# Fifth stage of a two-layer decoder: exponentials of the two key halves are added before the product with the column of ones

## The chip, the cores and the metric

The kernel runs on one core of a Trainium2 chip. Times are device microseconds of one launch; the time of a kernel is the median of its runs. Engines are called TensorE (PE in the profile; PEld is its loading of weights), VectorE (DVE), ScalarE (ACT), GpSimd (POOL) and SyncE (SP, which only issues transfers here).

## The reference

Two decoder layers, six steps, over x of 8 batches of 256 tokens and 256 features in fp32; each step adds its result to x and normalises. Steps 1, 2, 4 and 5 are attention with 16 heads of 16 features (1 and 5 differ in masks; 2 and 5 take keys and values from a context), step 3 is a mixture of four experts, step 6 of eight. The change is in step 5:

```python
logits = jnp.einsum('bhqd,bhkd->bhqk', q, k) / jnp.sqrt(jnp.asarray(dh, q.dtype))
logits = logits + neg[:, None, :, :]
attn = jax.nn.softmax(logits, axis=-1)
attn = attn * group_prob[:, None, :, :]
out = jnp.einsum('bhqk,bhkd->bhqd', attn, v)
```

The softmax is divided by the sum of its exponentials over the 256 keys *before* the product with group_prob. So two things are summed over keys for each head and query: exponential x group_prob x value (16 features), and the plain exponential (the divisor).

## The kernel before, in words

**Stages.** An Item (40 of them) is one batch in one of the five attention or projection stages; the fifth stage is items 32 to 39. Per item there are two groups g of 8 heads, and per group two parities par of 4 heads r. All matrices are fp32 unless a name says bf16.

**One group of the fifth stage.** score_rows makes scores with queries on the partitions; VectorE reduces them to row maxima (mrow), max_rows turns these with TensorE and folds them into q. weights(it, g, par) then makes scores with keys on the partitions: two tiles res[0], res[1] of [128, 2, 512] (tag pt, 6 buffers), each with two heads; the 512 columns of a head are 256 queries for the first 128 keys, then 256 queries for the second 128 keys. ScalarE writes the exponentials into them. In this stage alone (it.masked), each tile is multiplied by the group probabilities (it.gT, part of the tile mg) into a tile pw, in two instructions of 128x1024, each on VectorE or GpSimd.

values(it, g, par) sums over the keys in PSUM (av_ps, read later as avT). TensorE is used in four columns of 32 (mode "columns"), one head r in each. For both key halves kc and the four heads, pw meets the values in vaug (8 products of 256 queries). Then, in this stage, the bare exponentials p meet onesel, a [128, 32] matrix that is 1 in column 16 and 0 elsewhere, and add the divisor to the same PSUM tile: again 2 key halves x 4 heads, 8 products. In the other stages the ones sit in vaug beside the values and no such products are needed. After both parities VectorE transposes (avT), takes the reciprocal (ri) and VectorE or GpSimd multiplies (on); a second transpose gives oT for the output projection.

**What sets the order.** Program records every operation (note, and pe for a group of TensorE instructions that stay together), with the engines that may run it: either("vector", "gpsimd") leaves the choice open. order() then lays out the whole kernel as a list: it follows a simulated clock with its own durations (function duration, lines 238 to 255; columns for TensorE), gives next what can start first, and picks for each operation the engine that is expected to end it first, with LEAN = 0.5 us added to VectorE's end. Among TensorE operations that could start within a short wait, the one of lowest rank goes; the rank is a due time, moved a little by a table of numbers, DRAWS: one number for each stretch of 25 us of due time, which seeds random shifts and chooses the hold (a penalty for changing the array's mode) and the wait of that stretch. Each engine executes its part of the list in order. Every recorded instruction shows as line 394 (or 419) in the profile, so groups are told apart by their tiles.

**Queues and neighbours.** In the fifth stage GpSimd also runs on, the bias of the residual (res), small steps of the layer norm, the masks (mg from mi) and the scatters of finished rows to slots, which the sixth step's experts load; these begin before the stage ends (xeT, h, w in the profile). SyncE issues all loads.

Of the kernel before, what the change touches and what calls it, by code (L numbers as in the profile page):

```python
# [21 lines left out]
ALU = mybir.AluOpType  # L22
# [6 lines left out]
B, S, D = 8, 256, 256  # L29
# [16 lines left out]
AHEAD, HOLD, LEAN, WAIT = 500, 1.0, 0.5, 0.6  # L46
STRETCH = 25.0
DRAWS = (
    4492, 0, 1957, 1835, 1496, 0, 91, 5789, 2392, 5451, 5841, 3357, 6082, 1933, 4381, 1902, 4765,
    2407, 5027, 1409, 0, 3899, 0, 1034, 0, 0, 1677, 2696, 3561, 1043, 3249, 1318, 5799, 5442, 4785,  # L50
    5199, 1355, 3729, 1195, 1519, 1668, 942, 4299, 0, 0, 0, 0, 0,
)
TURN, SWITCH, SIGNAL, EARLY, RATE = 0.11, 0.2, 0.12, 40.0, 0.35e6

# [8 lines left out]
def columns(n, count=1):  # L63

    return count * n * 1.69e-3
# [208 lines left out]
class Program:  # L274
# [160 lines left out]
    def _close(self, op):  # L435
# [25 lines left out]
        op.pre.discard(op.idx)  # L461
        op.behind -= op.pre | {op.idx}

    def order(self):

        ops = self.ops
# [37 lines left out]

        rank_of, hold, wait = list(due), [HOLD] * len(ops), [WAIT] * len(ops)
        draws = {k: random.Random(1000 * k + n) for k, n in enumerate(DRAWS) if n}
        for op in ops:
            k = int(due[op.idx] // STRETCH)  # L510
            if k in draws:
                n = DRAWS[k]
                rank_of[op.idx] += (0.25, 0.5, 1.0, 2.0)[n % 4] * (2.0 * draws[k].random() - 1.0)
                hold[op.idx] = (0.5, 1.0, 2.0, 4.0)[n // 4 % 4]
                wait[op.idx] = (0.2, 0.3, 0.6, 1.0)[n // 16 % 4]
        left = [len(op.pre) + len(op.behind) for op in ops]
        begun = [0.0] * len(ops)
        end = [None] * len(ops)
# [1 line left out]
        ready = [i for i, n in enumerate(left) if n == 0]  # L520
        oldest, result = 0, []
        self.clock = []

        def places(op, now):

# [36 lines left out]
        def division(op):  # L562

            if op.mode == "any":
                return ("columns" if mode == "rows" else mode or "full",) * 2
            if op.mode == "rows, full":
                return ("full", "rows") if mode == "full" else ("rows", "full")
            return op.mode, op.mode

        while ready:  # L570
            choices = []
            for i in ready:
                op = ops[i]
                if i > oldest + AHEAD:
                    continue
                here = places(op, free.get(op.alts[0][0], 0.0))
                if here is None:
                    continue
                t0 = max([here[0]] + [begun[p] for p in op.behind])
                opts = []  # L580
                for e, f, d in op.alts:
                    t = t0
                    for p in op.pre:
                        if ops[p].ran != e or ops[p].lag:
                            t = max(t, end[p] + SIGNAL + (0.15 if ops[p].mode else 0.0))
                        else:
                            t = max(t, end[p])
                    t = max(t, free.get(e, 0.0))
                    if e == "sync":
                        t = max(t, due[i] - EARLY)  # L590
                    if e == "all":

                        t = max(free.values())
                    if op.mode:
                        first, then = division(op)
                        d += SWITCH * ((first != mode) + (first != then))
                    opts.append((t + d + (LEAN if e == "vector" else 0.0), t, d, e, f))
                fin, t, d, e, f = min(opts, key=lambda o: o[:3])
                rank = rank_of[i] + (hold[i] if op.mode and division(op)[0] != mode else 0.0)
                choices.append((t, rank, i, op, d, e, f, here[1]))  # L600
            if not choices:
                raise RuntimeError(f"operation {oldest} of {len(ops)} cannot be given")
            best = min(choices, key=lambda c: c[:3])
            if best[3].mode:

                best = min(
                    (c for c in choices if c[3].mode and c[0] <= best[0] + wait[best[2]]), key=lambda c: c[1:3])
            t, _, _, op, d, e, f, found = best
            i = op.idx
            if op.mode:  # L610
                first, then = division(op)
                op.split, op.flip = op.mode == "any" and first == "columns", (first, then) == ("full", "rows")
                mode = then
            op.ran = e
            if e == "all":
                for k in free:
                    free[k] += d
            else:
                free[e] = t + d
            begun[i], end[i] = t, t + d  # L620
            if op.lag:
                wire = max(wire, t + d + 1.3) + op.bytes / RATE
                end[i] = max(t + d + op.lag, wire + 0.9)
            for b, where in zip(op.new, found):
                for n in where:
                    lanes[b.key][n] = b
                b.at = where[0]
                taken[b.key] += not b.loose
            ready.remove(i)
            for j in op.post + op.ahead:  # L630
                left[j] -= 1
                if left[j] == 0:
                    ready.append(j)
            while oldest < len(ops) and (end[oldest] is not None or ops[oldest].alts[0][0] == "sync"):
                oldest += 1
            result.append(f)
            self.clock.append((t, t + d, e, i))
        return result


@with_exitstack
def decoder_kernel(ctx: ExitStack, tc: tile.TileContext, a: dict, out: bass.AP):
# [552 lines left out]
    def weights(it, g, par):  # L1195

        ps = [psum_s("st_ps") for _ in range(2)]
        res = [work.tile([P, 2, 512], F32, tag="pt", name="pt", bufs=6) for _ in range(2)]
        with nc.pe(columns(S, 1.75 if it.causal else 2) + (0.9 if it.masked else 0.0), "rows", res):
            for kc in range(2):  # L1200
                q0 = P if (it.causal and kc == 1) else 0
                for r in range(4):
                    rows32 = slice(32 * r, 32 * r + 32)
                    nc.tensor.matmul(
                        ps[r // 2][:, r % 2, kc * S : kc * S + S - q0],
                        lhsT=it.k[par][rows32, g, kc * P : (kc + 1) * P], rhs=it.q[par][rows32, g, q0:],
                        start=masks_last if it.masked and kc == 0 else not it.masked,
                        stop=masks_first if it.masked and kc == 1 else not it.masked,
                    )
            if it.masked:  # L1210
                with nc.whole():
                    for r in range(4):
                        nc.tensor.matmul(
                            ps[r // 2][:, r % 2, :], lhsT=identb, rhs=it.mk.rearrange("p k q -> p (k q)"),
                            start=masks_first, stop=masks_last,
                        )
        n = S + P if it.causal else 2 * S
        for t, p in enumerate(res):
            nc.scalar.activation(p[:, :, :n], ps[t][:, :, :n], AF.Exp)
            if it.causal:  # L1220
                d = p.rearrange("p r (b x) -> p r b x", b=2)[:, :, :, :P]

                nc.gpsimd.affine_select(
                    out=d, in_=d, compare_op=ALU.is_ge, fill=0.0, base=0,
                    pattern=[[0, 2], [0, 2], [1, P]], channel_multiplier=-1,
                )
        it.p[g, par] = res
        if it.masked:
            w = big("pw").rearrange("p (t r x) -> p t r x", t=2, r=2)
            gb = it.gT.rearrange("p k q -> p (k q)").unsqueeze(1).to_broadcast([P, 2, 512])  # L1230
            for t in range(2):
                nc.either("vector", "gpsimd").tensor_tensor(w[:, t], res[t], gb, ALU.mult)
            it.pw[g, par] = [w[:, 0], w[:, 1]]

    def values(it, g, par):
# [3 lines left out]
        ps = it.av  # L1239
        p = it.p.pop((g, par))  # L1240
        w = it.pw.pop((g, par)) if it.masked else p
        with nc.pe(columns(S, (1.5 if it.causal else 2) * (2 if it.masked else 1)), "columns"):
            for kc in range(2):
                q0 = P if (it.causal and kc == 1) else 0
                for r in range(4):
# [4 lines left out]
                        start=(kc == 0), stop=(kc == 1 and not it.masked),  # L1250
                    )
            if it.masked:
                for kc in range(2):
                    for r in range(4):
                        nc.tensor.matmul(
                            ps[32 * r : 32 * r + 32, par, :], lhsT=onesel,
                            rhs=p[r // 2][:, r % 2, kc * S : (kc + 1) * S], start=False, stop=(kc == 1),
                        )
        if par == 1:
            return  # L1260
        t = own_tile("avT", [P, 2, 8, 32], bufs=1)
# [990 lines left out]
```

## Time and profile before

| What | us |
|---|---|
| Median of 3 runs (lowest to highest) | 1420.42 (1420.22 to 1422.8) |
| The profiled execution, device time | 1426.34 |
| Its span, first to last instruction | 1424.3 |
| TensorE busy in the span | 1338.7 |
| VectorE busy | 903.0 |
| ScalarE busy | 618.9 |
| GpSimd busy | 598.5 |
| Fifth stage: first and last product with onesel begin at | 1029.5 and 1254.9 |
| Mean granted TensorE clock (a share of full speed) | 0.982 |

A group's line gives engine, operation, written tile <- read tiles, the shape (partitions x elements) and the count, then busy us, mean ns of one, and the engine's idle time just before such instructions with what ended it. A timeline's line gives start and length in us, engine, operation and count, with idle time before it in brackets. A stretch's line gives its bounds and length, then busy us and records (x) of each engine. Ends of matmuls are modelled and their spans overlap the next ones', so starts are the surer measure.

### The profile page before, as it was taken

What the parts mean: (1) busy time and instruction counts of PE and PEld (TensorE: products, weight loads), DVE (VectorE), ACT (ScalarE), POOL (GpSimd) and SP (SyncE); (2) the same over time, 40 slices, a digit from 0 to 9 for tenths busy, and PEclk for the clock granted to TensorE, in tenths of its full rate; (3) what the DMA queues carried; (4) which work ended last, traced back from release to release, by engine and by line L of the source; (5) the groups of instructions that cost most, each with busy time, mean ns of one, the idle gap of its engine ahead of it and who ended that gap; (6) DMA issues with size and microseconds to landing.
All of it is one profiled execution on the core that took longest, in us unless ns stands there. A gap on an engine that the chain in (4) does not pass through costs nothing. (4 is left out here: it accounts for less than half of the span.)

```text
span 1424.3 us, 34194 instructions
## 1 busy us (share of the span) xinstructions
PE 1338.7 (94%) x14418; PEld 907.7 (64%) x14448; DVE 903.0 (63%) x1813; ACT 618.9 (43%) x968; POOL 598.5 (42%) x979
## 2 busy tenths in 40 slices
PE   8999999999999988999899979999999999999995
PEld 5777666666666655757565645556566666577774
DVE  5777888778878875000230669987767878964332
ACT  3546575655655434222231354646443344432120
POOL 3446542314454665100260446672345556552222
PEclk9999999999999989999999989999999999999998
DMA  2210010400190013200320000021003103176500
GB/s 88 69 34 14 11 48 18 164 1 2 62 406 32 32 35 108 78 15 17 88 72 24 16 19 26 24 75 44 11 17 115 51 17 112 53 209 199 163 14 13
DMA packets 60753, 92.48 MB, mean 65 GB/s; under 512 B 6482, under 2 KB 49491, under 8 KB 59568
## 3 DMA queue, kind: packets, MB, share of 16 engines
q1 hardware_dynamic: 55792, 78.78, 17.0%
q0 software_dynamic: 4800, 11.41, 2.5%
q8 instruction: 118, 1.93, 0.6%
q14 instruction: 43, 0.35, 0.1%
HBM read 58.56 MB, written 32.28 MB: 64 GB/s over the span
## 5 line engine op out<-in xcount | busy, mean ns | idle before, releaser
L394 ACT ACTIVATE pt<-banks 128x1024 f32<-128x1024 f32 (+1 forms) x320 | 283.3, 937 | 226.0 <-PE banks L394 206.9
L394 DVE TENSOR_REDUCE mrow<-banks 128x4 f32<-128x1024 f32 (+1 forms) x320 | 342.6, 1109 | 58.9 <-PE banks L394 56.8
L394 PE MATMUL banks<-q,k 32*128 32x256 f32 (+1 forms) x2560 | 185.5, 382 | 11.1 <-PEq L343 5.0
L394 PE MATMUL banks<-k,q 32*128 32x256 f32 (+1 forms) x2560 | 187.3, 379 | 8.3 <-DVE mrow L394 6.8
L394 PEld LDWEIGHTS banks<-q,k 32*128 32x128 f32 x2560 | 128.3, 187 | 66.6 <-issue 39.5
L394 PEld LDWEIGHTS banks<-k,q 32*128 32x128 f32 x2560 | 129.3, 187 | 56.1 <-issue 20.2
L394 PE MATMUL banks<-pt,vaug 128*32 128x256 f32 (+1 forms) x2048 | 118.0, 361 | 4.5 <-DVE mrow L394 2.6
L394 POOL TENSOR_SCALAR_AFFINE_SELECT pt<-pt 128x512 f32<-128x512 f32 x128 | 81.4, 642 | 93.5 <-ACT pt L394 90.6
L394 POOL TENSOR_TENSOR on<-avT,ri 128x256 f32<-128x256 f32 x56 | 35.3, 631 | 180.2 <-DVE ri L394 147.6
L394 POOL TENSOR_TENSOR pw<-pt,mg 128x1024 f32<-128x1024 f32 x29 | 75.5, 2604 | 62.6 <-ACT pt L394 62.4
L394 PEld LDWEIGHTS banks<-pt,vaug 128*32 128x32 f32 x2048 | 58.8, 110 | 52.5 <-issue 14.9
L394 POOL DMA_INDIRECT got<-answers,where x32 | 31.2, 975 | 144.5 <-DMA xr<-sent 124.3
L394 PE MATMUL banks<-hid,big 128*128 128x512 f32 (+1 forms) x240 | 86.8, 521 | 0.0
L394 PE MATMUL banks<-xe,big 128*128 128x512 f32 (+1 forms) x216 | 82.4, 538 | 1.1 <-DVE xe L394 1.1
L394 ACT ACTIVATE hid<-banks 128x1024 f32<-128x1024 f32 (+1 forms) x39 | 34.3, 881 | 112.3 <-PE banks L394 112.2
L394 DVE STREAM_TRANSPOSE avT<-banks 128x512 f32<-128x512 f32 x80 | 56.8, 710 | 32.0 <-PE banks L394 22.3
L394 PE MATMUL banks<-xeT,w 128*128 128x320 f32 (+2 forms) x352 | 72.3, 362 | 1.8 <-DVE h L394 1.8
L394 DVE TENSOR_SCALAR xe<-banks,c_cols 128x512 f32<-128x512 f32 (+1 forms) x8 | 4.9, 613 | 108.8 <-PE banks L394 108.8
L394 PE MATMUL banks<-w,h 128*128 128x256 f32 (+1 forms) x384 | 72.2, 381 | 1.2 <-ACT h L394 1.2
L394 DVE SCALAR_TENSOR_TENSOR q<-banks,c_cols,q 128x256 f32<-128x256 f32 x160 | 69.0, 469 | 2.4 <-PE banks L394 2.2
L394 PEld LDWEIGHTS banks<-hid,big 128*128 128x128 f32 x240 | 45.5, 190 | 38.9 <-issue 36.8
L394 POOL TENSOR_SCALAR is_t<-ln_mv 128x2 f32<-128x2 f32 (+1 forms) x64 | 12.6, 197 | 133.9 <-DVE ln_mv L394 126.2
(247 smaller groups left out, 2392.4 us busy)
## 6 DMA issues: line engine op xcount, KB each, us to landing
w<-in_fw SPq DMA_DIRECT2D x16, 1024.0 KB, 6.9
sent<-zero SPq DMA_DIRECT2D x8, 1024.0 KB, 10.3
answers<-zero SPq DMA_DIRECT2D x8, 768.0 KB, 15.7
xr<-sent SPq DMA_DIRECT2D x20, 256.0 KB, 4.3
wa_w_s<-in_w_s SPq DMA_DIRECT2D x4, 1024.0 KB, 7.6
answers<-y SPq DMA_DIRECT2D x20, 192.0 KB, 2.4
slots<-empty SPq DMA_DIRECT2D x4, 645.0 KB, 3.3
xT<-in_xT SPq DMA_DIRECT2D x8, 256.0 KB
```

The lines of the kernel that those rows point to most:

```text
L394: made = getattr(getattr(self.nc, engine), name)(*[real(v) for v in args], **{k: real(v) for k, v in kw.items()})
```

## The change

In weights, after each product with the group probabilities, the second key half of the exponentials is added onto the first, in place, on VectorE or GpSimd (128 x 2 x 256 elements a tile). In values the products with onesel then run over the first half only: 4 instead of 8 in a call. The planner's price of the group falls from 4 to 3 columns(S).

The planner changes too, for all stages. The stretch of 25 us is now counted in TensorE work already given, no longer in an operation's due time; hold and wait are those of the present stretch for every operation; the random shift of the rank is one of 1009 by the operation's index, and may be off altogether (far = 0). DRAWS has 43 other numbers. Neither adds or removes instructions of another kind, but the order of work and the choice of engine can differ anywhere in the kernel.

```diff
 DRAWS = (
-    4492, 0, 1957, 1835, 1496, 0, 91, 5789, 2392, 5451, 5841, 3357, 6082, 1933, 4381, 1902, 4765,
...
+    50055, 14529, 7074, 30090, 1834, 0, 16611, 8237, 58962, 8718, 64962, 36059, 7299, 40069, 60251,
...
@@ order @@
-        rank_of, hold, wait = list(due), [HOLD] * len(ops), [WAIT] * len(ops)
-        draws = {k: random.Random(1000 * k + n) for k, n in enumerate(DRAWS) if n}
-        for op in ops:
-            k = int(due[op.idx] // STRETCH)
-            if k in draws:
-                n = DRAWS[k]
-                rank_of[op.idx] += (0.25, 0.5, 1.0, 2.0)[n % 4] * (2.0 * draws[k].random() - 1.0)
-                hold[op.idx] = (0.5, 1.0, 2.0, 4.0)[n // 4 % 4]
-                wait[op.idx] = (0.2, 0.3, 0.6, 1.0)[n // 16 % 4]
+        def drawn(k):
+            n = self.draw(k)
+            if not n:
+                return [0.0] * 1009, HOLD, WAIT
+            r, far = random.Random(1000 * k + n), (0.0, 0.5, 1.0, 2.0)[n % 4]
+            moved = [far * (2.0 * r.random() - 1.0) for _ in range(1009)]
+            return moved, (0.5, 1.0, 2.0, 4.0)[n // 4 % 4], (0.2, 0.3, 0.6, 1.0)[n // 16 % 4]
...
-                rank = rank_of[i] + (hold[i] if op.mode and division(op)[0] != mode else 0.0)
+                rank = due[i] + moved[i % 1009] + (hold if op.mode and division(op)[0] != mode else 0.0)
...
+            if op.mode:
+                work += op.alts[0][2]
+                if work >= (stretch + 1) * STRETCH:
+                    stretch += 1
+                    moved, hold, wait = drawn(stretch)
@@ weights @@
             for t in range(2):
                 nc.either("vector", "gpsimd").tensor_tensor(w[:, t], res[t], gb, ALU.mult)
+
+                half = res[t][:, :, :S]
+                nc.either("vector", "gpsimd").tensor_tensor(half, half, res[t][:, :, S:], ALU.add)
@@ values @@
-        with nc.pe(columns(S, (1.5 if it.causal else 2) * (2 if it.masked else 1)), "columns"):
+        with nc.pe(columns(S, 3 if it.masked else 1.5 if it.causal else 2), "columns"):
...
             if it.masked:
-                for kc in range(2):
-                    for r in range(4):
-                        nc.tensor.matmul(
-                            ps[32 * r : 32 * r + 32, par, :], lhsT=onesel,
-                            rhs=p[r // 2][:, r % 2, kc * S : (kc + 1) * S], start=False, stop=(kc == 1),
-                        )
+                for r in range(4):
+                    nc.tensor.matmul(
+                        ps[32 * r : 32 * r + 32, par, :], lhsT=onesel, rhs=p[r // 2][:, r % 2, :S],
+                        start=False, stop=True,
+                    )
```

## The prediction

> **What bounds the kernel now.** I read the page's slices first, then the busy time in stretches of the fifth stage, then the costly groups there, and last the timelines of VectorE and GpSimd beside TensorE's. The page:
>
> ```profile
> span 1424.3 us, 34194 instructions
> PE 1338.7 (94%) x14418; PEld 907.7 (64%) x14448; DVE 903.0 (63%) x1813; ACT 618.9 (43%) x968; POOL 598.5 (42%) x979
> ```
>
> TensorE carries the kernel. The averages hide the stage, so here is the fifth stage alone (first product with the values to the last), cut in its steady part and its end; columns are length, then busy time and records of PE, PEld, DVE, ACT, POOL, then clock and DMA:
>
> ```profile
> 1028.00:1220.00 192.00, 189.81 (x2057) 124.32 (x2076) 150.23 (x276) 75.35 (x110) 104.01 (x106) 1.00 0.18 61
> 1220.00:1258.00 38.00, 35.87 (x444) 21.87 (x442) 35.44 (x86) 18.36 (x28) 25.39 (x29) 1.00 0.39 128
> ```
>
> In the steady part TensorE works 189.8 of 192 us (98.9%) at clock 1.00, VectorE 78%, GpSimd 54%. In the last 38 us, where routing of the next stage comes in, VectorE is at 93% and TensorE has already fallen to 94%. So work taken off TensorE counts in full in the first part; in the second VectorE is as full as TensorE. The groups of the stage (stretch 1012 to 1258; busy, mean ns | idle before):
>
> ```profile
> L394 POOL TENSOR_TENSOR pw<-pt,mg 128x1024 f32<-128x1024 f32 x29 | 75.5, 2604 | 62.6 <-ACT pt L394 62.4
> L394 DVE TENSOR_TENSOR pw<-pt,mg 128x1024 f32<-128x1024 f32 x35 | 49.9, 1431 | 14.0 <-ACT pt L394 13.7
> L394 PE MATMUL banks<-pt,onesel 128*32 128x256 f32 x512 | 33.5, 379 | 0.0
> ```
>
> **What is removed.** Four of eight products with onesel in each of 32 calls of values (8 batches, 2 groups, 2 parities). An fp32 product shows as two records, so x512 is 256 products and 128 go. Their price is read from the starts on TensorE's timeline:
>
> ```profile
> 1107.19 1.07 PE L394 MATMUL banks<-pw,vaug 128*32 128x256 f32 x16
> 1108.08 1.05 PE L394 MATMUL banks<-pt,onesel 128*32 128x256 f32 x16
> 1108.95 1.05 PE L394 MATMUL banks<-pw,vaug 128*32 128x256 f32 x16
> ```
>
> Sixteen records take 0.87 us from start to start (the printed 1.05 holds a tail that overlaps the next group). Half of that is 0.43 us a call, 32 x 0.43 = 13.8 us, all on the path: 26 calls (11.2 us) fall in the steady part, 6 (2.6 us) in the end. Halving the row's busy time would give 16.7 us; I keep 13.8, as the starts hold no tail twice.
>
> **What is added.** 64 additions of 128x512 fp32, both inputs in SBUF, two per weights call. No row is this operation. On VectorE the nearest is the sum of the residual, 128x512, at 683 ns (one input is PSUM); the mask product at twice the width takes 1.22 us undisturbed. I take 0.68 us; from below 0.62, from above 0.68 plus a wait priced next. On GpSimd the residual bias, 128x512 from SBUF, takes 1217 ns; from below 1.04 (the square, one tensor read twice). I take 1.2 us. The plan gives an operation to the engine that it expects to end it first: by its formulas VectorE 0.685 plus the lean of 0.5 is 1.185, GpSimd 1.224, a tie, so the freer engine wins. All on VectorE would be +43.5 us, all on GpSimd +77; I take half and half: VectorE +21.8, GpSimd +38.4. Even that leaves GpSimd below 80% of the stage.
>
> **The wait between the two engines.** The two timelines around 1124 us, VectorE and GpSimd:
>
> ```profile
> 1117.60 2.75 DVE L394 TENSOR_TENSOR pw<-pt,mg 128x1024 f32<-128x1024 f32 x1
> 1124.18 3.48 DVE L394 TENSOR_TENSOR pw<-pt,mg 128x1024 f32<-128x1024 f32 x1
> ```
>
> ```profile
> 1116.88 2.38 POOL L394 TENSOR_TENSOR pw<-pt,mg 128x1024 f32<-128x1024 f32 x1
> 1124.16 2.42 POOL L394 TENSOR_TENSOR pw<-pt,mg 128x1024 f32<-128x1024 f32 x1 [4.90 <-ACT pt L394]
> ```
>
> Both VectorE products end 1.1 us after GpSimd's end (1120.35 after 1119.26, 1127.66 after 1126.58): they stood still until GpSimd was done. The Trainium skill, "SBUF — State Buffer", section "Who interferes with whom", says so as a rule: a VectorE instruction with two SBUF inputs and a GpSimd instruction that reads SBUF shut each other out for the whole instruction, and a reduction never takes part. The new addition is exactly of this kind, and it comes free when the other half's product runs on GpSimd. By the rule at its worst each VectorE addition waits out a 2.4 us product: 32 x 2.4 = 77 us on VectorE, and the change is lost. By the row it is far less: the 35 products took 49.9 us where 35 x 1.22 is 42.7, so 7.2 us or 0.2 us each, because the plan mostly put reductions of PSUM on VectorE beside GpSimd's product. The plan doesn't know the lock, so this is luck of order; I take the row's 0.2 us, 32 x 0.2 = 6.4 us, ends 0 and 2.4.
>
> What stands behind a blocked addition is VectorE's queue: the row maxima (mrow), whose end TensorE waits for, for 27 us in the whole trace but under 5 us in this stage. On GpSimd the additions push back the normalisation of the heads, the small steps of the layer norm and the scatters to slots; all of these have microseconds of cover (GpSimd waited 62 us for its products' inputs). SyncE gets nothing new.
>
> **The sum.** The fullest 20 us stretches of VectorE in which TensorE still kept up (890 to 910: VectorE 19.02, TensorE 19.67) show 95.1%; I use that as VectorE's ceiling. Steady part: TensorE's floor is 192 - 11.2 = 180.8 us; VectorE is 150.2 + 26 x (0.68 + 0.2) = 173.1 us, which at 95.1% needs 182.0 us. So -10.0 us. End: VectorE's 35.4 us leave no room. With 3 of its 12 additions on VectorE (+2.6, 38.1 us) and 9 on GpSimd (+10.8, 36.2 us) it needs about 38.1 / 0.951 = 40 us: not -2.6 but +2 at most; the last group of weights has no cover (TensorE waited 1.5 us for pw at 1253), and its addition of 0.7 to 1.2 us lies inside these 2 us. I take +1.5. The new wait of TensorE for the additions costs nothing before that: GpSimd's product ended at 1152.36 and the product with the values that needs it began at 1158.84, 6.5 us later, against 0.7 to 3.6 us of addition. If that cover went, each us of lateness would stop TensorE in order, with the next scores behind it.
>
> After the stage nothing takes the gain back: from 1258 on the one transfer that TensorE waits for is a load of rows, 1.5 us, and never the expert weights, so the rest moves up with the stage.
>
> The new draws reorder all stages, and the stretch rule is new. They add no instruction; what they can move is TensorE's idle time, 85.6 us in all, of which 79 lie outside the stage. Nothing in the trace gives a sign. I put 0, with +/-5 us (about 6% of that idle time) for the range.
>
> Total: -10.0 + 1.5 = -8.5 us. The profiled execution took 1426.34 us (span 1424.3 and 2.0 around it), 5.9 above the median of the runs; 1426.3 - 8.5 = 1417.8 there is 1420.4 - 8.5 = **1411.9 us** as a median.
>
> **Rivals.**
> - *TensorE keeps all of it* (24%). VectorE never becomes the limit, because the additions fill its 22% of gaps or go mostly to GpSimd. Then -13.8, and up to -5 from the order: 1402 to 1407. For it: VectorE at 78% in the steady part, GpSimd at 54%. Against: the end stretch.
> - *VectorE takes it all back* (11%). Same mechanism as mine, with waits near 0.46 us an addition: (197.4 + 21.8 + 32 x 0.46) / 0.951 = 246 us, the old length of 1012 to 1258. About 1420.
> - *The lock makes it slower* (23%). VectorE's additions fall under GpSimd's products, since product 1 starts on GpSimd as product 0 ends on VectorE and frees addition 0. From 0.46 us of mean wait on it loses; at 0.8 us, a third of a product, 244.8 / 0.951 = 257.4 us, that is +11: 1432. For it: the two rows above. Against: 0.2 us in the same stage.
> - That the change doesn't do what it says I hold for nearly excluded: the sum over keys is linear, and the products go whatever the plan does.
>
> **The numbers.** Forecast 1408 to 1417: 42%. A measurement of this kernel tells about 0.2% (2.8 us) from no change. Faster, below 1417.6: 24 + 42 = 66%. Same: 11%. Slower: 23%. The range goes from 1400 (full gain, order +5 in favour and a little more) to 1427, which leaves out the worst half of the lock's cases, some 13%, and some 4% below.
>
> **What would show it.** onesel at x256 and about 17 us busy; 64 additions (pt<-pt) near 0.68 us on VectorE and 1.2 us on GpSimd, about half each. VectorE at 90 to 95% from 1028 on, TensorE still over 96%. A mean of VectorE's additions over 1.1 us, or TensorE waiting for mrow by 10 us or more in the stage, would prove the lock's case; VectorE under 88% with TensorE over 98% the first rival. I am wrong outright if the time before 1000 us has moved by more than 5 us: then the order, not the additions, made the result.

## The result and the profile after

The changed kernel takes 1438.11 us (median of 4 runs, 1434.99 to 1439.68) against 1420.32 us (1419.55 to 1422.8) for the kernel before on the same chip: a ratio of 1.0109 [1.0092, 1.0126], 15.5 us slower at 1420 (the two medians lie 17.8 us apart; the text goes by the ratio). The forecast, 1411.9 us, had the wrong sign. The profiled execution took 1439.68 us.

The head of the page of the changed kernel:

```profile
span 1438.0 us, 33744 instructions
PE 1333.2 (93%) x14151; PEld 909.1 (63%) x14180; DVE 946.1 (66%) x1846; ACT 614.3 (43%) x966; POOL 658.4 (46%) x1010
```

Against before, TensorE's busy time fell by only 5.5 us although 128 products went; VectorE gained 43.1 us and GpSimd 59.9 us. The span grew by 13.7 us. The first product with onesel began 4.5 us later (1034.0 after 1029.5), the last 10.6 us later (1265.5 after 1254.9), and the end came 13.7 us later: in these two executions 4.5 us were lost ahead of the stage, 6.1 in it, 3.1 behind it. What lies ahead of the stage differs a good deal between executions: runs 4 to 6 below have the order of the changed kernel and ran on one chip, and their first product with onesel began at 1036.9, 1031.0 and 1025.8 us. So 4.5 us there says little; the length of the stage is the surer measure.

The stage should have become shorter. From the first to the last product with the values, before and after (length, busy us and records of PE, PEld, DVE, ACT and POOL, granted clock, DMA):

```profile
1028.60:1254.00 225.40, 221.08 (x2437) 142.60 (x2464) 181.35 (x345) 91.58 (x134) 127.23 (x132) 1.00 0.20 67
1033.10:1265.10 232.00, 216.62 (x2201) 138.29 (x2227) 207.69 (x350) 91.80 (x138) 193.94 (x174) 0.98 0.21 70
```

The stage of the changed kernel in its steady part and its end:

```profile
1033.00:1220.00 187.00, 178.87 (x1805) 116.38 (x1828) 163.85 (x279) 75.03 (x111) 154.62 (x139) 0.99 0.18 62
1220.00:1268.00 48.00, 39.44 (x416) 22.64 (x412) 46.56 (x83) 19.03 (x31) 40.41 (x38) 0.93 0.32 104
```

TensorE, at 98.9% and 94% before, is at 95.7% in the steady part and 82% in the end, where the granted clock is 0.93. VectorE stands at 87.6% and 97%, GpSimd at 83% and 84%. The groups behind that (idle before them after the bar):

```profile
L394 POOL TENSOR_TENSOR pt<-pt 128x512 f32<-128x512 f32 x53 | 70.8, 1353 | 3.7 <-DVE pw L394 3.1
L394 DVE TENSOR_TENSOR pt<-pt 128x512 f32<-128x512 f32 x11 | 19.3, 1755 | 4.0 <-POOL pw L394 3.8
L394 PE MATMUL banks<-pt,onesel 128*32 128x256 f32 x256 | 20.9, 390 | 1.8 <-POOL pt L394 1.5 <-DVE pt L394 0.3
```

The onesel products are halved as meant. But the additions went 53 to GpSimd and 11 to VectorE, and those 11 took 1755 ns each where 680, or 880 with the wait, were expected.

How one of them stops TensorE is seen around 1155 us. VectorE:

```profile
1155.31 2.88 DVE L394 TENSOR_TENSOR pt<-pt 128x512 f32<-128x512 f32 x1 [2.06 <-POOL pw L394]
1158.12 0.53 DVE L394 TENSOR_SCALAR q<-banks,c_cols,sh 128x256 f32<-128x256 f32 x1
```

GpSimd over the same microseconds:

```profile
1152.88 2.40 POOL L394 TENSOR_TENSOR pw<-pt,mg 128x1024 f32<-128x1024 f32 x1
1155.25 1.25 POOL L394 TENSOR_TENSOR pt<-pt 128x512 f32<-128x512 f32 x1
1156.47 1.17 POOL L394 TENSOR_TENSOR res<-x,ba_b_s 128x512 f32<-128x512 f32 x1
```

and TensorE:

```profile
1156.77 0.60 PE L394 MATMUL banks<-k,q 32*128 32x256 f32 x4
1159.88 1.13 PE L394 MATMUL banks<-k,q 32*128 32x256 f32 x12 [2.52 <-DVE q L394]
```

VectorE's addition first waits 2.06 us at the head of the queue until GpSimd's product has read the tile. Then it lasts 2.88 us: GpSimd goes from the product to its own addition, and from that to the residual bias, without a gap, and VectorE is done 0.55 us after the last of these (1158.19 after 1157.64). Nearly all of the 2.88 us was standing still: the median addition of run 4 takes 0.68 us. The q of the next scores stands behind it, and TensorE waits 2.52 us for q. The two stretches around this wait (clock is the last column but two):

```profile
1155.00:1160.00 5.00, 2.43 (x28) 1.42 (x28) 4.02 (x5) 1.92 (x5) 4.12 (x5) 1.00 0.07 26
1160.00:1165.00 5.00, 5.00 (x44) 2.17 (x48) 4.55 (x10) 1.18 (x2) 3.74 (x2) 0.66 0.00 1
```

The wait is followed by 5 us in which TensorE runs at 0.66 of its clock: by estimate (5 x 0.34) it costs about 1.7 us more. In steps of 1 us from 1160 on, the granted clock reads 1.00, 0.60, 0.50, 0.50, 0.69 and 1.00: it is halved for some 3.4 us, beginning about 1 us after TensorE has resumed.

### The profile page after: what moved, and what is told of

It reads as the page before. It is cut to its first block, busy times and chain, and to the rows that moved or that the text cites. A ratio compares the mean times of both kernels' runs of the same rounds, so it can differ in the third digit from the quotient of the medians.

```text
span 1438.0 us, 33744 instructions
## 1 busy us (share of the span) xinstructions
PE 1333.2 (93%) x14151; PEld 909.1 (63%) x14180; DVE 946.1 (66%) x1846; ACT 614.3 (43%) x966; POOL 658.4 (46%) x1010
## 5 line engine op out<-in xcount | busy, mean ns | idle before, releaser
L394 PE MATMUL banks<-k,q 32*128 32x256 f32 (+1 forms) x2560 | 190.5, 380 | 18.5 <-DVE q L394 6.5
L394 PE MATMUL banks<-q,k 32*128 32x256 f32 (+1 forms) x2560 | 182.0, 380 | 11.2 <-PEq L343 4.3
L394 PEld LDWEIGHTS banks<-k,q 32*128 32x128 f32 x2560 | 132.5, 188 | 62.6 <-issue 19.0
L394 PE MATMUL banks<-pt,vaug 128*32 128x256 f32 (+1 forms) x2048 | 114.9, 356 | 8.4 <-DVE mrow L394 5.3
L394 POOL TENSOR_TENSOR on<-avT,ri 128x256 f32<-128x256 f32 x42 | 27.1, 645 | 122.4 <-DVE ri L394 90.7
L394 DVE TENSOR_SCALAR xe<-banks,c_cols 128x256 f32<-128x256 f32 (+1 forms) x7 | 4.2, 598 | 119.0 <-ACT xe L394 60.0
L394 POOL TENSOR_TENSOR pw<-pt,mg 128x1024 f32<-128x1024 f32 x26 | 69.3, 2664 | 27.0 <-ACT pt L394 26.8
L394 PE MATMUL banks<-xeT,w 128*128 128x320 f32 (+2 forms) x352 | 75.8, 375 | 0.1
L394 POOL TENSOR_TENSOR pt<-pt 128x512 f32<-128x512 f32 x53 | 70.8, 1353 | 3.7 <-DVE pw L394 3.1
```

The lines of the kernel that those rows point to most:

```text
L394: made = getattr(getattr(self.nc, engine), name)(*[real(v) for v in args], **{k: real(v) for k, v in kw.items()})
```

## The experiments

Theory after the result ("port"): VectorE's instructions with two SBUF inputs and GpSimd's shut each other out, and the additions fill that shared resource. Rivals: the new order and draws ("order"); the sheer load of either engine; the halved products being worth less than 13.8 us. Ratios are to the kernel before on the same chip, with 95% intervals; its own median differed from chip to chip (1406 to 1423 us), so microseconds are given as ratio x 1420.

**1. The products alone.** Order of before on every engine; onesel over the first key half only, nothing added.

```diff
-                for kc in range(2):
-                    for r in range(4):
-                            rhs=p[r // 2][:, r % 2, kc * S : (kc + 1) * S], start=False, stop=(kc == 1),
+                for r in range(4):
+                        ps[32 * r : 32 * r + 32, par, :], lhsT=onesel, rhs=p[r // 2][:, r % 2, :S],
```

> The order of before on every engine, but the products with onesel run over the first key half only and nothing is added (the divisor leaves out the second half of the keys). It prices what is removed, alone. If TensorE is the limit of the stage: 13.8 us less than before, about 1406.6. If VectorE were already the limit there, under half of that: above 1413.

0.9950 [0.9936, 0.9963]: -7.1 us, half of 13.8. Its stage, from the first to the last product with onesel:

```profile
1009.00:1228.00 219.00, 210.78 (x2185) 135.69 (x2204) 183.20 (x355) 92.40 (x135) 127.29 (x133) 0.99 0.22 72
```

Over the same marks before took 225.5 us (1029.50 to 1255.00) with TensorE busy 221.2: TensorE lost 10.4 us of work, but 3.9 of that became idle time. The longest waits in this stage are for VectorE (mrow 1.7, pw 1.5, avT 1.0 us), which is at 84%.

**2. No products with onesel at all** (the ones are left in vaug instead), order of before.

```diff
-                        nc.tensor.matmul(
-                            ps[32 * r : 32 * r + 32, par, :], lhsT=onesel,
...
-                nc.gpsimd.memset(it.vv[:, :, :, HD:], 0.0)
+                nc.gpsimd.memset(it.vv[:, :, :, HD:], 1.0)
```

> The order of before with no product with onesel at all (the ones stand in vaug as in the other stages, so the divisor is the sum of the exponentials after their product with the group probabilities). Twice the removal of the first experiment, 27.7 us of TensorE by starts. TensorE alone is the limit: 0.979 to 0.983 of before. Theory that VectorE and the port already limit the stage once TensorE is relieved: hardly more than the first experiment, 0.988 to 0.995.

0.9925 [0.9903, 0.9946]: -10.7 us for twice the work. By the ratios the first half was worth 7.1 and the second 3.6, but their intervals overlap, and the stage itself got shorter by 6.7 and then by 5.7 us (225.4, 218.7, 213.0). That the second half is worth less is not shown.

**3. The additions are planned but not run**, order and draws of after.

```diff
                 nc.either("vector", "gpsimd").tensor_tensor(half, half, res[t][:, :, S:], ALU.add)
+                nc.ops[-1].alts = [(e, lambda: None, d) for e, _, d in nc.ops[-1].alts]
```

> The order of after on every engine, only the 64 additions are left out (the divisor leaves out the second half of the keys). Theory that the additions do the harm (through the read port that VectorE and GpSimd share, or through GpSimd's queue): at least 20 us less than after, 1410 to 1417. Rival, the new order and draws do it: stays above 1430.

0.9982 [0.9967, 0.9997]. The additions themselves thus cost 1.0109 - 0.9982 = 1.27%, 18 us (3 either way; at least 20 were expected), in this order; and the new order without them is 4.5 us worse than run 1. By the length of the stage the additions cost 16.1 us:

```profile
1020.90:1236.80 215.90, 210.59 (x2197) 136.34 (x2223) 180.14 (x342) 91.98 (x138) 123.48 (x124) 1.00 0.21 70
```

**4. The additions all on VectorE**, order of after (53 moved):

```diff
+                op = nc.ops[-1]
+                op.alts = [(e, op.alts[0][1], d) for e, _, d in op.alts]
```

> The order of after, all 64 additions given to VectorE (53 moved over from GpSimd, each at its place in the order). Theory of the shared read port: an addition holds the port 0.68 us on VectorE and 1.2 us on GpSimd, so the port gets 28 us free: faster than after, 1.000 to 1.006 of before. Rival, VectorE's own queue is what is full (207 us busy of 232 in the stage, and +36 here): slower than after, 1.015 or more.

1.0126 [1.0109, 1.0143]. The wait of each is small now, but VectorE has all the work:

```profile
L394 DVE TENSOR_TENSOR pt<-pt 128x512 f32<-128x512 f32 x64 | 53.8, 843 | 1.9 <-POOL pw L394 1.7
```

In the stage (241.5 us) VectorE is busy 226.4, 94%. This is neither theory's number: a load problem of VectorE, with little lock.

**5. All on GpSimd** (11 moved), alts[1] in place of alts[0].

> The order of after, all 64 additions given to GpSimd (11 moved over from VectorE). Port: 6 us more of port time, but VectorE stands still less: like after, 1.007 to 1.013. Rival, GpSimd's queue (193 us busy of 232 in the stage, and +13 here) delays the products: 1.014 or more. Rival, VectorE's queue: faster than after, under 1.006.

1.0095 [1.0078, 1.0112], as the port theory had it: no addition is left on VectorE, and the loss stays. In the stage VectorE's busy time is 198.9 us here (1030.2 to 1261.3) and 180.1 in run 3, although it runs no addition in either. Four of its groups in run 3:

```profile
L394 DVE TENSOR_REDUCE mrow<-banks 128x4 f32<-128x1024 f32 x52 | 61.2, 1216 | 0.1
L394 DVE TENSOR_TENSOR lg<-banks,mx 128x16 f32<-128x16 f32 x6 | 1.0, 175 | 0.2
L394 DVE TENSOR_TENSOR oh<-val,vm 128x16 bf16<-128x16 f32 x5 | 0.9, 173 | 0.1
L394 DVE TENSOR_TENSOR s<-to,s 128x2 uint32<-128x2 f32 x5 | 0.6, 122 | 0.0
```

and the same four here, counted 1 us further:

```profile
L394 DVE TENSOR_REDUCE mrow<-banks 128x4 f32<-128x1024 f32 x52 | 61.1, 1215 | 0.3 <-PE banks L394 0.3
L394 DVE TENSOR_TENSOR oh<-val,vm 128x16 bf16<-128x16 f32 x6 | 4.7, 790 | 0.2
L394 DVE TENSOR_TENSOR s<-to,s 128x2 uint32<-128x2 f32 x5 | 2.2, 445 | 0.0
L394 DVE TENSOR_TENSOR lg<-banks,mx 128x16 f32<-128x16 f32 x6 | 1.0, 174 | 0.2
```

The reduction and the step with a PSUM input (banks) take what they took; the two whose inputs both lie in SBUF take 4.6 and 3.6 times as long. Of the rows with two SBUF inputs not all do: to<-to,keep (128x2) stays at 212 and 207 ns, so it depends on what GpSimd runs at that moment.

**6. GpSimd as occupied, but reading nothing.** Each of GpSimd's 53 additions is replaced by two memsets of the same half; VectorE's 11 stay.

```diff
+                def twice(half=half):
+                    for _ in range(2):
+                        nc.nc.gpsimd.memset(half.ap(), 1.0)
+                op.alts = [op.alts[0], ("gpsimd", twice, op.alts[1][2])]
```

> The order of after; GpSimd's 53 additions are replaced by two memsets of the same tile half with 1.0, which write the same tile but read nothing (the divisor is not the sum of the exponentials). GpSimd stays as busy, within a fifth, and the same waits stand; only the reads are gone. Port: most of the loss goes, 1.003 or less. Rival, GpSimd's queue or the wait of TensorE for the added tiles: 1.008 or more.

0.9985 [0.9969, 1.0000]: the loss is gone. GpSimd's share and VectorE's additions:

```profile
L1249 POOL MEMSET pt<- 128x512 f32 x106 | 54.6, 526 | 7.7 <-DVE pw L394 4.3
...
L394 DVE TENSOR_TENSOR pt<-pt 128x512 f32<-128x512 f32 x11 | 8.4, 760 | 2.9 <-POOL pw L394 2.6
```

The 11 additions take 760 ns here and 1755 in the changed kernel, and oh is back at 173 ns. The memsets keep GpSimd busy for 54.6 us, 23% less than the 70.8 of the additions, a little outside what was set, so occupation alone is not wholly excluded by this run; but run 5, with more of it (200.4 us in the stage against 193.9), was no slower than the changed kernel. The stage takes 218.5 us here, 2.6 more than without any addition and 13.5 less than in the changed kernel.

**7. Old planner, new stage:** planner and draws of before, the change laid out anew (DRAWS and order() as before, the rest as after).

> The additions and halved products with the planner and the draws of before (laid out anew by it). Additions do the harm: slower than before again, 1428 to 1442. Rival, new order and draws: the forecast gain appears, 1407 to 1415.

1.0132 [1.0104, 1.0160]: the change loses without the new planner too.

**8. New planner, old stage:** planner and draws of after, weights() and values() of before.

> The planner and draws of after, the fifth stage as in before (no additions, eight products). Additions do the harm: near before, 1420 to 1430 (draws made for another kernel may cost a few us). Rival, new order and draws: 1433 or more.

1.0099 [1.0061, 1.0137], 1434 at 1420: wide, but it is the number of the rival, and there is no addition in this kernel. Its stage takes 227.1 us, only 1.7 more than before, and what follows as long as before. So the order of after costs something of its own, and most of that must lie ahead of the fifth stage; runs 12 and 14 return to it.

**9. No draws at all** (DRAWS = ()), the kernel of before, and **10.** the same with the change:

> Before with an empty table of draws (the planner's plain order): the base for the next run. A table fitted to its kernel is worth 5 to 20 us: 1.003 to 1.014 of before.

1.0207 [1.0186, 1.0229]: the draws of before are worth 29 us, about twice what I thought. Run 13 puts the part of the fifth stage and what follows at 3.5 us, so by estimate some 26 lie ahead of it.

> The additions and the halved products with the planner of before and an empty table of draws. Additions do the harm in any order: at least 8 us slower than the run with no draws and no additions. Rival, the harm lies in the order that the draws picked: as fast as that run or faster.

1.0177 [1.0151, 1.0203]. In a plain order the change is 0.3% (4 us) faster than run 9, which is not clear of noise, as the intervals overlap; but it is not the 8 us or more slower that were expected, so "it harms in any order" fell. The lock is there all the same:

```profile
L390 POOL TENSOR_TENSOR pt<-pt 128x512 f32<-128x512 f32 x52 | 68.9, 1340 | 7.5 <-DVE pw L390 4.2 <-PE banks L390 3.1
...
L390 DVE TENSOR_TENSOR pt<-pt 128x512 f32<-128x512 f32 x12 | 17.5, 1462 | 1.7 <-POOL pw L390 1.3
```

It seems to be paid for out of idle time: VectorE is at 86% of this stage, TensorE idles 8.9 us in it (15.4 in the changed kernel), and the granted clock is 1.00.

**11. The plain order with the additions not run** (edit of run 3 on run 10):

> The order of the run with no draws and the change, but the additions are left out (the divisor leaves out the second half of the keys). If an addition costs the same in any order: 16 to 20 us faster than with them, near 1.005 of before. If their cost hangs on where they stand in the order: less than 10 us faster, 1.011 or more.

1.0121 [1.0083, 1.0159]. The additions cost 0.56%, 8 us, here, and 18 in the order of after; the halved products are worth 0.86%, 12 us. Both are uncertain by some 6 us. By the length of the stage the additions cost 10.3 us (212.1 to 222.4), and the halved products are worth 16.0 (228.1 to 212.1).

**12 to 14. Draws in the first four stages only** (the first 33 numbers), so that the fifth is plain: the change under the old planner, the kernel of before, and the changed kernel.

```diff
-        draws = {k: random.Random(1000 * k + n) for k, n in enumerate(DRAWS) if n}
+        draws = {k: random.Random(1000 * k + n) for k, n in enumerate(DRAWS[:33]) if n}
```

> The change with the planner of before; its draws hold up to the start of the fifth stage (first 33 stretches), from there none. Order theory (the draws of the fifth stage make the additions dear): within 4 us of before, 0.997 to 1.003, against 1.013 with all draws of before. Rival, additions cost about 18 us anywhere: 1.010 or more.

1.0012 [1.0000, 1.0024]; with all draws (run 7) it was 1.0132. The old draws of this one stage cost the changed stage 17 us.

> Before, with its draws only up to the fifth stage: the control for the change in a plain fifth stage, without additions. 1.000 to 1.004 of before; the change in the same order of earlier stages should come out up to 4 us faster than this.

1.0025 [1.0011, 1.0038]: to the stage before, the same draws were worth 3.5 us. In a plain fifth stage the change is thus worth -0.13%, about 2 us, which these intervals cannot tell from nothing.

> After, with its draws only up to the fifth stage (first 33 stretches) and none from there. Order theory: 6 us or more faster than after, 1.002 to 1.006 of before. Rival, additions cost the same anywhere: 1.009 or more.

1.0075 [1.0057, 1.0094], between the two expectations. The new draws of the stage cost 5 us; 10.7 us stay. Run 12 has the same change and the same plain stage (222.2 and 222.4 us) and differs only in the planner and the draws ahead of it: 0.63%, 9 us (3 either way), is lost there.

**15. Half of the additions, on GpSimd, unplanned:** order of before, parity 1 only, each right behind its product.

```diff
+                if par == 1:
+                    op, half = nc.ops[-1], res[t][:, :, :S]
+                    op.alts = [(e, lambda f=f, t=t: (f(), nc.nc.gpsimd.tensor_tensor(
+                        res[t].ap()[:, :, :S], res[t].ap()[:, :, :S], res[t].ap()[:, :, S:], ALU.add)), d)
+                        for e, f, d in op.alts]
```

> The order of before; only parity 1 gets additions, both on GpSimd right behind their products and unplanned, and only its products with onesel are halved (32 additions, 6.9 us of TensorE by starts). Lock theory: additions where the plan has not kept the port free cost more than they save: 1.002 to 1.010. Rival, half the dose fits into GpSimd's free time: 0.996 to 0.999.

1.0102 [1.0076, 1.0129], at the edge of what was expected, but mostly for another reason:

```profile
L1236 POOL TENSOR_TENSOR pt<-pt 128x512 f32<-128x512 f32 x32 | 42.7, 1336 | 52.5 <-DVE pw L394 48.9 <-PE banks L394 1.2 <-DVE off L394 1.2
```

GpSimd stood 49 us before these additions, until VectorE's product had read the tile, and its later work stood behind them. This run doesn't size the port.

**16. The rounding on ScalarE instead.** If the shared port is the price, the onesel products should be made cheaper by an engine outside it: ScalarE (41% busy in the stage before) rounds the exponentials to bf16 in place after pw is made; all eight products are kept, in bf16, so the divisor is a sum of rounded exponentials. Planner and draws of before, laid out anew.

```diff
+                nc.scalar.copy(narrow(res[t]), res[t])
...
-    onesel = const.tile([P, 32], F32, name="onesel")
+    onesel = const.tile([P, 32], BF16, name="onesel")
...
-                            rhs=p[r // 2][:, r % 2, kc * S : (kc + 1) * S], start=False, stop=(kc == 1),
+                            rhs=narrow(p[r // 2])[:, r % 2, kc * S : (kc + 1) * S], start=False, stop=(kc == 1),
```

> The planner and draws of before, no additions: ScalarE rounds the exponentials to bf16 in place once the product with the group probabilities is made, and all eight products with onesel run in bf16 (laid out anew by the planner). ScalarE doesn't use the shared port and has over 100 us free in the stage; TensorE's eight products shrink by more than half. Port theory: faster than before, 0.990 to 0.998, and no slower than with the additions left out. Rival, any step between product and sum delays the stage: 1.003 or more.

0.9956 [0.9939, 0.9973]: faster than both kernels.

```profile
L394 ACT CAST pt<-pt 128x1024 bf16<-128x1024 f32 x64 | 66.3, 1044 | 35.9 <-POOL pw L394 18.9 <-DVE pw L394 16.5
...
L394 PE MATMUL banks<-pt,onesel 128*32 128x256 bf16 x256 | 13.7, 273 | 0.2 <-ACT pt L394 0.2
```

The eight products take 13.7 us of TensorE (33.5 in fp32), and ScalarE's 66 us lie beside. Once begun, none of ScalarE's 64 roundings is held up: they took 1027 to 1063 ns each.

**17. The same rounding in the order of before**, unplanned behind each product.

> The order of before on every engine, with the bf16 rounding on ScalarE put behind each product and the sum over the keys in bf16. Nothing of it uses the shared port; TensorE's products with onesel shrink at least as much as in the first experiment. Port theory: 0.991 to 0.997. Rival, ScalarE's queue, which now waits for the products before its next exponentials: 1.000 or more.

1.0148 [1.0121, 1.0175]: the rival was right. ScalarE's waits in the stage:

```profile
ACT pt L1235 <- POOL pw L394: 31.8, 24, 3.0
ACT pt L1235 <- DVE pw L394: 25.3, 29, 3.6
```

57 us in which the next exponentials stood behind a rounding that waited for its product. The planner's place for the instruction is what makes run 16.

**18. Rounding on ScalarE, fifth stage without draws** (runs 16 and 12 joined).

> The version with the bf16 rounding on ScalarE, with the draws of before only ahead of the fifth stage. If what matters there is the removal of TensorE work without use of the shared port, it stays faster than before in this order too: 0.993 to 0.998, and 5 us or more faster than before in a plain fifth stage (1.0025). Rival, its gain was luck of the draws: 1.000 or more.

0.9931 [0.9904, 0.9958], 1412.74 us against 1423.21 on that chip: the best version found. Its interval overlaps that of run 16.

**The same runs by stage.** From the first to the last product with the values, and from there to the last instruction, one execution each (a little other work of TensorE moves across these bounds):

| Kernel | Order of the fifth stage | Stage, us | Behind it, us |
|---|---|---|---|
| Before | old draws | 225.4 | 170.3 |
| Run 1: products halved only | old draws | 218.7 | 168.4 |
| Run 7: the change | old draws | 238.7 | 180.4 |
| Run 8: old stage | new draws | 227.1 | 170.4 |
| Run 3: additions not run | new draws | 215.9 | 172.5 |
| Run 6: memsets | new draws | 218.5 | 170.9 |
| Changed kernel | new draws | 232.0 | 172.9 |
| Run 9: old stage | plain | 228.1 | 169.6 |
| Run 13: old stage | plain | 229.1 | 168.4 |
| Run 11: additions not run | plain | 212.1 | 174.4 |
| Runs 10, 12, 14: the change | plain | 222.4, 222.2, 222.4 | 173.6, 174.5, 173.7 |

In a plain order the change shortens the stage by 5.7 and 6.9 us (runs 9 to 10, 13 to 12), not far from the 8.5 of the forecast; but 4.0 and 6.1 us come back behind it, about 2 of each as TensorE work that has moved there.

## Why the prediction failed

In short: the additions were allowed 5.3 us (13.8 less the forecast's 8.5) and cost 18. The step that failed is the wait between VectorE and GpSimd, put at 0.2 us for each new instruction on VectorE. Besides, the halved products gave 7.1 us and not 13.8, and the new order, put at 0, cost 4.5.

**What is removed: the work was right, "all on the path" held only in part.** The records halved as said. By themselves the halved products were worth 7.1 us in the old order (run 1), not 13.8; in a plain one 12 (run 11), from which 13.8 cannot be told. Taking off the whole 27.7 us in the old order gives 10.7.

**What is added: the split and the GpSimd price.** 53 to 11, not half and half; the plan's lean of 0.5 us and VectorE's fuller queue probably decided the tie, which no run tests. GpSimd took 1353 ns against 1.2 us forecast. So GpSimd got 70.8 us and not 38.4, VectorE 19.3 and not 28.2: less on VectorE than forecast, and still slower.

**The wait between the engines: the term that failed.** I took 0.2 us per VectorE addition from the row of pw; measured are 1755 - 680 = 1.07 us, beyond the 0.46 us at which my third rival turns, and I had said that a mean over 1.1 us for an addition would prove the lock's case: it was 1.755. With only 11 additions that is 12 us of waiting, less than the 14.7 (32 x 0.46) of that rival. But the term was also drawn too narrowly. It counted waits of VectorE's *new* instructions; GpSimd's new reads also hold VectorE's old ones, such as oh, which took 173 ns in run 3:

```profile
L394 DVE TENSOR_TENSOR oh<-val,vm 128x16 bf16<-128x16 f32 x5 | 4.2, 847 | 0.1
```

From run 3 to the changed kernel VectorE's busy time in the stage grows by 27.6 us (180.1 to 207.7). Of that, 16.7 are the nine additions that fall in the stage, and about 11 are old instructions that last longer: oh, s, on, off, ex and at, all with both inputs in SBUF. With these it is some 23 us of waiting. The products pw lose next to nothing as a group (1450 ns in run 3, 1462 here); in the worst case seen one of them, 1.2 us undisturbed, lasts 6.1 us. VectorE:

```profile
1244.92 6.10 DVE L394 TENSOR_TENSOR pw<-pt,mg 128x1024 f32<-128x1024 f32 x1
1251.06 1.64 DVE L394 TENSOR_TENSOR pt<-pt 128x512 f32<-128x512 f32 x1
```

GpSimd beside it:

```profile
1245.08 2.49 POOL L394 TENSOR_TENSOR pt<-pt 128x512 f32<-128x512 f32 x2
1247.53 2.41 POOL L394 TENSOR_TENSOR pw<-pt,mg 128x1024 f32<-128x1024 f32 x1
1250.02 2.13 POOL L394 TENSOR_TENSOR pt<-pt 128x512 f32<-128x512 f32 x1
```

VectorE's product gets its turn only when GpSimd's ends at 1249.94, and finishes 1.08 us later: it stood still through three instructions of GpSimd in a row. GpSimd's next addition meanwhile takes 2.13 us instead of 1.25, and VectorE's addition ends 0.55 us after that one.

**The step behind it: two budgets that share one thing.** "Even that leaves GpSimd below 80% of the stage" and "VectorE at 95.1%" were checked apart. GpSimd's reads and VectorE's instructions with two SBUF inputs shut each other out, so their times have to be added. An estimate from undisturbed durations (2.4 and 1.2 us a product, 1.25 and 0.68 an addition, and what GpSimd does besides, some 40 to 54 us in these stages): before, 29 x 2.4 + 35 x 1.2 = 112 and 40 to 50 make 152 to 162 of 225 us, about 70%. After, 26 x 2.4 + 38 x 1.2 + 53 x 1.25 + 11 x 0.68 = 182 and 42 to 54 make 224 to 236 of 232 us: full. The sum was to be had from the profile of before, and it would have shown the risk. It doesn't decide the outcome: by the same estimate run 10, in the plain order, has 19 x 2.4 + 45 x 1.2 + 52 x 1.25 + 12 x 0.68 = 173 and 42 to 54, 215 to 227 of 222 us, just as full, and its stage got shorter.

**VectorE's ceiling was not the bound.** It is 89.5% busy in the stage (207.7 of 232.0), below the 95.1% used, and TensorE waits nevertheless: its idle time in the stage goes from 4.3 to 15.4 us. Lateness at single places decides, not the mean. What TensorE waited for in the changed kernel's stage (us, times, longest):

```profile
PE banks L394 <- DVE q L394: 4.7, 5, 2.5
PE banks L394 <- DVE pw L394: 2.4, 1, 2.4
PE banks L394 <- DVE mrow L394: 1.9, 2, 1.3
PE banks L394 <- POOL pt L394: 1.5, 2, 0.9
```

**The end: the place right, the size not measured by itself.** I took +1.5 us for the end stretch. The last groups show the lack of cover as foreseen, with waits for additions:

```profile
1235.34 1.05 PE L394 MATMUL banks<-pw,vaug 128*32 128x256 f32 x16
1237.31 0.62 PE L394 MATMUL banks<-pt,onesel 128*32 128x256 f32 x4 [0.92 <-POOL pt L394]
1238.53 0.62 PE L394 MATMUL banks<-pt,onesel 128*32 128x256 f32 x4 [0.59 <-POOL pt L394]
```

"6.5 us of cover" held elsewhere (1.8 us of wait for additions in all), and the larger waits were for q, pw and mrow, as listed above; seen at 1155 and 1254 us, such an instruction stands behind a late one on VectorE or is late itself. The forecast had the mrow queue as the place, not q, and its sign of 10 us of waiting for mrow did not come.

**The granted clock was left out.** Mean 0.982 before, 0.974 after, 0.98 over the stage: by estimate 2% of TensorE's 217 us there is about 4 us of the loss, a cost of the same waits. At the end of the stage, where the first products of the sixth begin, the clock is low for 8 us:

```profile
1256.00:1260.00 4.00, 2.44 (x24) 0.62 (x24) 3.86 (x13) 0.22 (x1) 3.12 (x5) 0.60 1.05 398
1260.00:1264.00 4.00, 3.84 (x20) 3.83 (x21) 3.90 (x3) 1.62 (x5) 3.92 (x3) 0.55 0.78 264
```

The Trainium skill, "TensorE: Matmul & The Clock Gate", section "Part 1: The HAM clock gate (the "warmup" mystery)", puts a halved clock after an idle window of about 3.4 us; here waits of 2.4 and 2.5 us were followed by stretches at 0.55 to 0.66, with the clock at 0.50 for part of them. The halving agrees; on the length of the wait the measurement decides, and shorter ones can be enough.

**Behind the stage.** "After the stage nothing takes the gain back" failed: 2.6 us more from the last product with the values to the end. Run 3, the same order without additions, has nearly the same (172.5 and 172.9 us), so this belongs to the order; in the plain order 4.0 and 6.1 us came back there. Beyond the TensorE work that moved, why is open.

**The draws.** "0, with +/-5 us" was too small. Ahead of the stage runs 12 and 14 put the loss at 9 us; the two profiles and runs 1 and 3 (the new order in all, 4.5 us) put it lower. I had said that over 5 us there would make me wrong outright, with the order as the cause. By runs 12 and 14 that happened, and yet the additions cost 18 us in one and the same order (run 3), so both are at work. Inside the stage the order also sets the price of the additions, 8 us in a plain order and 18 in that of after (10.3 and 16.1 by the length of the stage), and the old draws made the change 17 us dearer (run 7 against run 12).

**The sum, from runs:** halved products in the old order -7.1, new order +4.5, additions +18.0 make +15.4 us; measured +15.5 (the terms are differences of runs, so they must close; what is new is their size). Against them the forecast had -13.8 for the products, 0 for the order and +5.3 for the additions: the price of the additions was the largest error. The mechanism was on record as the third rival, at 23%; its price there, +11, was short by 4, and that it came so near is in part luck, as it left out the order's share.

**Open:** which collisions the draws of after bring together and the plain order spares. The runs show that order sets the price, not a rule for a good one. How much of the loss lies ahead of the stage is bounded only roughly: about 3 us by runs 1 and 3 (4.5 in all, less what the table shows from the stage on), 9 by runs 12 and 14. And the share that GpSimd's occupation has beside its reads is bounded by runs 5 and 6, not measured apart.

## What to carry to other kernels

Before work goes to VectorE or GpSimd, add up GpSimd's time and VectorE's instructions with two SBUF inputs as one resource; near 100% waits of several times an instruction can come, whether they cost anything depends on the order, and the small all-SBUF steps of other stages pay too. Relief for a full TensorE is better sought on an engine outside that pair (here ScalarE: 0.9956 to 0.9931). Work taken off TensorE need not come back in full: in the old order about half did (7.1 of 13.8 us). An order fitted to one kernel must be tested apart from the change it comes with: the same edit measured from no difference to +1.3% with the order alone.

## What was not expected of the hardware

- The lock falls hardest, in proportion, on some of the smallest instructions: two steps of 128x2 and 128x16 went from 122 and 173 ns to 755 and 847 ns on average.
- GpSimd's memsets, which read nothing, nearly left VectorE's two-input instructions alone: 760 ns an addition beside 106 of them.
- A TensorE wait of 2.5 us was enough for a granted clock of 0.66 in the next 5 us.
- The product with onesel took 273 ns a record in bf16 and 379 in fp32, of which fp32 needs two: 13.7 against 33.5 us for the same sums.
